# Half of the second batch's keys projected at the first batch's second norm, and the first attention begun with half of v

## The chip, the core and the metric

The kernel runs on one core of a Trainium2 chip. A core has five engines that work side by side, each through its own queue of instructions: TensorE (PE in the profile; its weight loads are PEld), VectorE (DVE), ScalarE (ACT), GpSimd (POOL) and SyncE (SP, which here only issues DMA transfers). They wait for one another by semaphores. The metric is the time of one execution on the device in microseconds (us). The kernel before took 3892.06 us in the median of three runs (3891.22 to 3893.94).

## What is computed

The input x has 8 batches of 1024 tokens (32 x 32) with 512 channels, in fp32. Two attention layers with a residual follow each other, each after a group norm over 32 groups of 16 channels and all tokens:

```python
# layer 0: 16 heads of 32 channels
qkv = _gn(x).reshape(B, N, C) @ w_qkv
attn = softmax((q * SCALE) @ k.T)           # per head, 1024 x 1024
x = x + (attn @ v) @ w_proj + b_proj
# layer 1: 4 heads of 128 channels, with relative positions
q, k, v = _gn(x) @ Wq * scale, _gn(x) @ Wk, _gn(x) @ Wv
attn = softmax(q @ k.T + rel_w + rel_h)     # the two terms come from q and pos_emb_w, pos_emb_h
x = x + (attn @ v) @ Wo
```

## The kernel before

**Products.** Every projection of a batch (512 x 512 weights times 512 channels x 1024 tokens) is done by a scheme with seven block products instead of eight (`seven`), twice per projection, for unit u = 0 and u = 1, each of which gives half of the output. So a projection is 14 products. One product is two chunks of 128 channels, each as four matmuls of 32 output columns side by side (`by_columns`, L312), for two halves where the output is in rows. The products of one unit come in the order `ORDER = [0, 5, 1, 4, 6, 2, 3]` and gather in three PSUM banks x, y and z; ACT copies two partial results into SBUF (p1, p7) and one out (c11), DVE does the adds a (L372), b (L380), c12 (L414) and c21 (L417), and POOL adds c22 (L421). The data side of the products are sums of quarters of x, made by `forms` (four DVE operations, L332 to L335): three of them lie in tiles of their own (`form1`, `form2`, `form4`, one buffer each), one in place. The weight side (differences of quarters of each weight matrix) is made once by `Matrix.add_up` (L146) and kept in DRAM; for the three matrices of the first batch's q, k and v it also stays in SBUF (`kept`).

**The stream of weights.** `Stream` follows a plan, a list of (matrix, rows or columns, unit). While a product of one unit runs, `ahead(i)` issues on SP the load of the same factor for the next unit, so weights are loaded seven products ahead (L194, L198).

**Attention 0** (`attention_0`) has 64 steps per batch: four groups of four heads, two halves of 512 queries, eight blocks j of 128 keys. `front` of a step does the scores of four heads into one PSUM tile ps, which has one buffer (L532), and ACT's exponential of it into e (L540, two buffers). `back` of the step before multiplies e with v into acc (L551) and adds e to the running sum es on DVE (L560 for the second block, L562 for the later ones). After the last block `finish` sums es over keys on PE (L572), and `normalise` turns it into reciprocals (L495 to L513) and multiplies q's place, where the output now lies, on POOL (L517).

**The order.** `side_by_side` runs attention 0 of batch b and, between its steps, draws the other work of the loop's turn b from a chain of generators in proportion to costs: a product counts 2, and a turn's `total` is spread over the 65 steps. In turn 0 this other work is `rest_of_first` (the second halves of q and k of batch 0), the loading and norm of batch 1 (`load`), and `before_0` of batch 1 (q, k, v: 42 products), with `other_sums`, the weight sums of five more matrices on POOL, put in after products 2, 9, 16, 23 and 30 of it. In turn 1 it is the output projection WP of batch 0 (`after_0`), its norm 1 (`norm_1`, with the scalings at L292), the projections of layer 1 (`second`), attention 1 (L647 to L670) and `before_0` of batch 2. Around the norm of turn 1 four entries of cost `ALONE = 4` are drawn with no product, and the first matmuls of `second` are kept in program order (`marked`). From turn 2 on, the norm lies between the products of WO of an older batch. What is drawn gives each instruction its rank; within an engine's queue an instruction can be put earlier when the ones ahead of it are not ready by the compiler's plan.

Before turn 0, `load_first` reads and norms batch 0, and `before_first` projects all of v and the first halves of q and k; only then the first attention begins.

**Room.** Large tiles (x, q, k, v, weight sums) share eight blocks of one pool (`BLOCKS = 8`).

Of the kernel before, what the change touches and what calls it, by code (L numbers as in the profile page):

```python
# [27 lines left out]
def quick_path(  # L28
# [138 lines left out]
    class Stream:  # L167
# [3 lines left out]
        def __init__(self, plan):  # L171
            self.plan = plan
            self.tiles = {}
            self.at = -1
            for i in ORDER:
                self.load(0, i)

        def load(self, n, i):
            if n >= len(self.plan):
                return  # L180
            m, rows, u = self.plan[n]
            if rows and u == 1:
                self.tiles[n, i] = self.tiles[n - 1, i]
                return
            got = []
            src = m.factor(i)
            if m.kept:
                got = [src[:, c, :] if rows else src[:, c, u * P : (u + 1) * P] for c in range(HC)]
                if i == ORDER[-1] and (u == 1 or rows):
                    m.kept = None  # L190
            elif rows:
                for c in range(HC):
                    t = mem.tile([P, HN], F32, tag="w", name=f"w_{m.name}_{n}_{i}_{c}", bufs=16)
                    nc.sync.dma_start(t, src[:, c, :])  # L194
                    got.append(t)
            else:
                t = mem.tile([P, HC, P], F32, tag="w", name=f"w_{m.name}_{n}_{i}", bufs=16)
                nc.sync.dma_start(t, src[:, :, u * P : (u + 1) * P])  # L198
                got = [t[:, c, :] for c in range(HC)]
            self.tiles[n, i] = got  # L200

        def unit(self, m, rows, u):
            self.at += 1
            assert self.plan[self.at] == (m, rows, u)

# [3 lines left out]

        def ahead(self, i):  # L210
            self.load(self.at + 1, i)

# [40 lines left out]

    def group_norm(st, xT, name, after=None):

# [35 lines left out]
        for cc in range(CC):  # L291
            nc.vector.tensor_scalar(  # L292
                xT[cc],
                xT[cc],
                mean[:, cc : cc + 1],
                rstd[:, cc : cc + 1],
                op0=ALU.subtract,
                op1=ALU.mult,
            )
            if cc % 2:  # L300
                yield 0


    in_place = [False]

    half_done = [None]

# [15 lines left out]

    def forms(x, name):


        a11, a12 = x[:, :HC, :NB], x[:, HC:, :NB]
        a21, a22 = x[:, :HC, NB:], x[:, HC:, NB:]
        s1, s2, s4 = [
            mem.tile([P, HC, NB], F32, tag=f"form{i}", name=f"f{i}_{name}", bufs=1) for i in (1, 2, 4)  # L330
        ]
        nc.vector.tensor_add(s1, a21, a22)  # L332
        nc.vector.tensor_sub(s2, s1, a11)
        nc.vector.tensor_sub(a21, a11, a21)
        nc.vector.tensor_sub(s4, a12, s2)  # L335
        return [a11, a12, s4, a22, s1, s2, a21]
# [4 lines left out]
    def seven(fs, u, rows, sink, name, hook=None):  # L341
# [4 lines left out]
        def product(out, i, start):  # L346
# [4 lines left out]
            else:  # L351
                for t in range(2):
                    for c in range(HC):
# [7 lines left out]
                        )  # L361
            stream.ahead(i)

# [7 lines left out]
        a = snapshot("es1", f"a_{name}")  # L371
        nc.vector.tensor_add(a, y, p1)  # L372
        sink.early(p1, a)
# [97 lines left out]

    def project_rows(fs, m, y, name, hook=None):

        for u in range(2):
            dst = [
# [42 lines left out]

    def attention_0(q, k, v, b):

        steps = [(m, h, j) for m in (0, 2, 1, 3) for h in range(NH) for j in range(NT)]
        state = {}
# [20 lines left out]
        def back(m, h, j, e):  # L543
            name = f"0_{b}_{m}_{h}_{j}"
            if j == 0:
                state["acc"] = psum.tile([P, NB], F32, tag="acc", name=f"acc_{name}", bufs=1)
                state["first"] = e
            acc = state["acc"]
            for r in range(HB):
# [4 lines left out]
                    e[:, r, :],  # L554
                    start=(j == 0),
                    stop=(j == NT - 1),
                )
            if j == 1:
                state["esum"] = mem.tile([P, HB, NB], F32, tag="es0", name=f"es_{name}", bufs=1)
                nc.vector.tensor_add(state["esum"], state["first"], e)  # L560
            elif j > 1:
                nc.vector.tensor_add(state["esum"], state["esum"], e)  # L562
            if j < NT - 1:
                return
# [193 lines left out]
    def before_first(st):  # L758

        fs = st["xn"]  # L760
        st["v"] = block("v0_0", [P, NT, C])
        yield from project_rows(fs, WV0, st["v"], "v0_0")
        st["q0"] = block("q0_0")
        st["q"] = chunks(st["q0"])
        st["k"] = chunks(block("k0_0"))
        yield from project_T(fs, WQ0, st["q"], "q0_0", (0,))
        yield from project_T(fs, WK0, st["k"], "k0_0", (0,))

    def rest_of_first(st):
# [4 lines left out]
    def before_0(b, st, hook=None):  # L774

        fs = st.pop("xn")
        st["q0"] = block(f"q0_{b}")
        st["q"] = chunks(st["q0"])
        yield from project_T(fs, WQ0, st["q"], f"q0_{b}")
        st["k"] = chunks(block(f"k0_{b}"))  # L780
        yield from project_T(fs, WK0, st["k"], f"k0_{b}")
        st["v"] = block(f"v0_{b}", [P, NT, C])
        yield from project_rows(fs, WV0, st["v"], f"v0_{b}", hook)

    def after_0(b, st, hook=None):

        fs = st.pop("ao0") if "ao0" in st else forms(st["q0"], f"ao0_{b}")
        x = st["x1"] = block(f"x1T_{b}")
# [9 lines left out]

    def norm_1(b, st, after=None):
        xT = chunks(st["x1"])  # L800
        st["kept"] = put_away(xT, f"1_{b}")
        yield from group_norm(st, xT, f"1_{b}", after)

# [57 lines left out]

    def side_by_side(first, rest, total):

        steps = CC * NH * NT + 1
        done = 0
        at = 0
        for _ in first:
# [25 lines left out]

    ALONE = 4

    WQ0, WK0, WV0 = [Matrix(w_qkv, i * C, f"qkv{i}") for i in range(3)]
    WP, WQ1, WK1 = Matrix(w_proj, 0, "p"), Matrix(Wq, 0, "q1"), Matrix(Wk, 0, "k1")
    WV1, WO = Matrix(Wv, 0, "v1"), Matrix(Wo, 0, "o")
    def units(m, rows=False):
        return [(m, rows, u) for u in range(2)]  # L900

    FIRST = units(WQ0) + units(WK0) + units(WV0, True)
    plan = units(WV0, True) + [(m, False, u) for u in range(2) for m in (WQ0, WK0)]
    for b in range(B + 1):
        if b >= 1:
            plan += units(WP)
        if b >= 2:
            plan += units(WO)
        if b >= 1:
            plan += units(WQ1) + units(WK1) + units(WV1, True)  # L910
        if b + 1 < B:
            plan += FIRST
    plan += units(WO)
# [22 lines left out]
    for b in range(B + 1):  # L936
# [11 lines left out]
        if last is not None:  # L948
            norm = norm_1(b - 1, last, (lambda: half_done[0]) if past is not None else None)
            rest.append(after_0(b - 1, last, forms_past if past is not None else None))  # L950
# [4 lines left out]
            else:  # L955
                rest.append(chain([ALONE], (cost + ALONE for cost in norm), marked()))
                total += 4 * ALONE
            rest.append(later(second, b - 1, last))
# [15 lines left out]
        if coming is not None:  # L974

            before = later(before_0, b + 1, coming, forms_0 if last is not None else None)
            rest.append(before if last is not None else woven(before, other_sums(), 2, 7))
            total += 3 * PRODUCT - (PRODUCT // 2 if last is not None else 0)
        if here is not None:
            side_by_side(attention_0(here["q"], here["k"], here["v"], b), chain(*rest), total)  # L980
# [495 lines left out]
```

## Time and profile before

| what | us |
|---|---|
| median of three runs | 3892.06 |
| span of the profiled execution | 3891.6 |
| PE busy / not busy in the span | 3809.4 / 82.2 |
| first matmul of the first projection | 25.66 |
| first scores of attention 0 of batch 0 | 79.08 |
| WP of batch 0 begins | 342.53 |
| layer 1's q of batch 0 begins | 420.20 |

In a line of the timeline the columns are start, duration, engine, line, operation, output and inputs, how often, and in brackets the idle time just before it and what ended it. In a line of a stretch they are its bounds, its length, and for each engine busy time and number of instructions, then the clock granted to TensorE (1.00 is full), the busy share of the DMA engines and GB/s. A line of waits has the total, the number and the longest.

### The profile page before, as it was taken

What the parts mean: (1) busy time and instruction counts of PE and PEld (TensorE: products, weight loads), DVE (VectorE), ACT (ScalarE), POOL (GpSimd) and SP (SyncE); (2) the same over time, 40 slices, a digit from 0 to 9 for tenths busy, and PEclk for the clock granted to TensorE, in tenths of its full rate; (3) what the DMA queues carried; (4) which work ended last, traced back from release to release, by engine and by line L of the source; (5) the groups of instructions that cost most, each with busy time, mean ns of one, the idle gap of its engine ahead of it and who ended that gap; (6) DMA issues with size and microseconds to landing.
All of it is one profiled execution on the core that took longest, in us unless ns stands there. A gap on an engine that the chain in (4) does not pass through costs nothing.

```text
span 3891.6 us, 79819 instructions
## 1 busy us (share of the span) xinstructions
PE 3809.4 (98%) x34478; PEld 1368.4 (35%) x34478; DVE 2515.8 (65%) x2905; ACT 1725.4 (44%) x1767; POOL 618.9 (16%) x400
## 2 busy tenths in 40 slices
PE   8999899999999999999999999999999999999998
PEld 3222244232442324432344323433234332334353
DVE  5767775577755867458674586646866568665544
ACT  2554553445435354344544445444453445553132
POOL 1341001121111210112110121111211112001101
PEclk9999999999999999999999999999999999999999
DMA  5231120133201422023220231202411033111401
GB/s 169 77 106 42 47 61 6 39 116 69 62 1 40 124 66 57 6 81 92 53 55 13 92 89 41 53 20 92 93 41 41 25 96 76 33 43 34 123 17 23
DMA packets 482984, 234.73 MB, mean 60 GB/s; under 512 B 269600, under 2 KB 461376, under 8 KB 481600
## 3 DMA queue, kind: packets, MB, share of 16 engines
q1 hardware_dynamic: 470992, 213.74, 20.4%
q0 software_dynamic: 2608, 13.70, 1.0%
q8 instruction: 274, 4.49, 0.5%
q10 hardware_dynamic: 9024, 2.10, 0.3%
q14 instruction: 86, 0.70, 0.1%
HBM read 170.72 MB, written 58.72 MB: 59 GB/s over the span
## 4 chain that ended last, share of the span: by engine, by line
PE 86%; DVE 7%; ACT 3%; issue 2%; POOL 1%; DMA 0%; SPq 0%; DVEq 0%; POOLq 0%; ACTq 0%
PE ps L532 12%; PE ps L647 11%; PE acc L659 11%; PE acc L551 10%; PE y_v L312 4%; PE y_k L312 4%; PE y_q L312 4%; PE ps L648 3%; PE x_v L312 3%; PE x_k L312 3%; PE x_q L312 3%; PE z_k L312 3%; PE z_v L312 3%; PE z_q L312 3%; ACT e L540 2%; DVE es L562 2%
## 5 line engine op out<-in xcount | busy, mean ns | idle before, releaser
L540 ACT ACTIVATE e<-ps 128x2048 f32<-128x2048 f32 x512 | 961.7, 1878 | 838.1 <-PE ps L532 624.0
L562 DVE TENSOR_TENSOR es<-es,e 128x2048 f32<-128x2048 f32 x384 | 892.1, 2323 | 422.7 <-ACT e L540 420.1
L532 PE MATMUL ps<-q,k 32*64 32x512 f32 x8192 | 577.1, 615 | 27.4 <-ACT e L540 27.4
L650 ACT ACTIVATE e<-ps 128x512 f32<-128x512 f32 x512 | 306.0, 598 | 572.2 <-PE ps L648 538.9
L551 PE MATMUL acc<-e,v 128*32 128x512 f32 x4096 | 547.3, 606 | 0.0
L647 PE MATMUL ps<-q,k 128*128 128x512 f32 x1024 | 525.0, 594 | 0.3 <-DVE posT L633 0.3
L659 PE MATMUL acc<-e,v 128*128 128x512 f32 x1024 | 521.9, 592 | 0.0
L517 POOL TENSOR_TENSOR q<-q,su 128x512 f32<-128x512 f32 x128 | 213.3, 1666 | 1596.1 <-DVE su L513 1551.3
L670 DVE TENSOR_TENSOR es<-es,e 128x512 f32<-128x512 f32 x384 | 290.7, 757 | 251.0 <-ACT e L650 248.9
L648 PE MATMUL ps<-posT,sel 128*128 128x512 f32 x512 | 406.7, 794 | 0.0
L647 PEld LDWEIGHTS ps<-q,k 128*128 128x128 f32 x1024 | 192.5, 190 | 251.2 <-issue 244.8
L532 PEld LDWEIGHTS ps<-q,k 32*64 32x64 f32 x8192 | 120.3, 130 | 422.7 <-issue 220.5
L659 PEld LDWEIGHTS acc<-e,v 128*128 128x128 f32 x1024 | 193.1, 189 | 146.8 <-issue 105.2
L551 PEld LDWEIGHTS acc<-e,v 128*32 128x32 f32 x4096 | 81.5, 108 | 413.2 <-issue 366.2
L560 DVE TENSOR_TENSOR es<-e,e 128x2048 f32<-128x2048 f32 x64 | 174.3, 2723 | 38.4 <-ACT e L540 38.4
L497 DVE STREAM_TRANSPOSE tu<-su 128x512 f32<-128x512 f32 x128 | 90.6, 708 | 128.8 <-ACT su L495 128.7
L495 ACT COPY su<-sums 128x512 f32<-128x512 f32 x128 | 75.1, 586 | 150.7 <-PE sums L572 78.0
L648 PEld LDWEIGHTS ps<-posT,sel 128*128 128x128 f32 x512 | 97.3, 190 | 122.5 <-issue 122.5
L633 DVE TENSOR_TENSOR posT<-pp,posT 32x512 fp32r<-32x512 f32 x128 | 112.0, 875 | 32.1 <-ACT posT L628 30.8
L668 DVE TENSOR_TENSOR es<-e,e 128x512 f32<-128x512 f32 x64 | 44.2, 690 | 134.8 <-ACT e L650 134.8
L421 POOL TENSOR_TENSOR k<-b_k,p_k 128x512 f32<-128x512 f32 x32 | 51.1, 1598 | 482.0 <-ACT p_k L386 480.0
L628 ACT CAST posT<-pp 32x512 fp32r<-32x512 f32 x128 | 106.0, 828 | 45.9 <-PE pp L615 44.8
(195 smaller groups left out, 4457.4 us busy)
## 6 DMA issues: line engine op xcount, KB each, us to landing
w_qkv<-ws_qkv SPq DMA_DIRECT2D x168, 128.0 KB, 2.5
d<-x0T SPq DMA_DIRECT2D x32, 512.0 KB, 3.5
x1T<-d SPq DMA_DIRECT2D x32, 512.0 KB, 5.2
d<-x1T SPq DMA_DIRECT2D x32, 512.0 KB, 3.6
x2T<-d SPq DMA_DIRECT2D x32, 512.0 KB, 6.1
w_qkv<-in_L_conv_w_qkv SPq DMA_DIRECT2D x126, 128.0 KB, 2.2
out<-ot SPq DMA_DIRECT2D x240, 64.0 KB, 2.0
xs<-in_x SPq DMA_DIRECT2D x224, 64.0 KB, 2.6
```

The lines of the kernel that those rows point to most:

```text
L312: ins = nc.tensor.matmul(out[columns, :], weights[:, columns], moving, start=start, stop=stop, skip_group_check=open_sum,)
L517: nc.gpsimd.tensor_tensor(dst, dst, su, op=ALU.mult)
L532: nc.tensor.matmul(ps[some, r, :], k[m][rows, j * P + 64 * i : j * P + 64 * i + 64], q[m][rows, h * NB : (h + 1) * NB], start=True, stop=True,
L540: nc.scalar.activation(e, ps, AF.Exp, scale=D0 ** -0.5)
L551: nc.tensor.matmul(acc[r * D0 : (r + 1) * D0, :], v[:, j, c0 : c0 + D0], e[:, r, :], start=(j == 0), stop=(j == NT - 1),)
L560: nc.vector.tensor_add(state["esum"], state["first"], e)
L562: nc.vector.tensor_add(state["esum"], state["esum"], e)
L647: nc.tensor.matmul(ps, k[h][:, keys], q[:, h, queries], start=True, stop=False)
L648: nc.tensor.matmul(ps, sel_flat[:, keys], posT[:, h, queries], start=False, stop=True)
L650: nc.scalar.activation(e, ps, AF.Exp, scale=1.0 / math.sqrt(D1))
L659: nc.tensor.matmul(acc, v[:, j, h * D1 : (h + 1) * D1], e, start=(j == 0), stop=(j == NT - 1),)
L670: nc.vector.tensor_add(state["esum"], state["esum"], e)
```

## The change

The plan of the stream now lists for every unit which factors it loads, and `ahead()` loads the next one of a flat list of all uses. The second half of v of batch 0 is no longer projected ahead of the first attention but between its first four steps, two products per step; in these four steps nothing else is drawn (`alone`), and all of batch 0 takes the key blocks in the order 0, 1, 4, 5, 2, 3, 6, 7. `before_0` of batch 1 leaves out the second half of k; this is projected in turn 1 after WP, with the norm of batch 0 woven between its products in place of the `ALONE` entries, and the norm's four scalings are queued on DVE behind the last add a (`begun`). Since x of batch 1 is still in use then, the forms of batch 0's attention output get a block in place of the form tiles.

```diff
         def load(self, n, i):
-            if n >= len(self.plan):
-                return
-            m, rows, u = self.plan[n]
-            if rows and u == 1:
+            m, rows, u, some = self.plan[n]
+            if rows and u == 1 and not m.kept:
                 self.tiles[n, i] = self.tiles[n - 1, i]
                 return
...
-        def ahead(self, i):
-            self.load(self.at + 1, i)
+        def ahead(self):
+            use = next(self.uses, None)
+            if use is not None:
+                self.load(*use)
...
-            nc.vector.tensor_scalar(
-                xT[cc],
-                xT[cc],
-                mean[:, cc : cc + 1],
-                rstd[:, cc : cc + 1],
-                op0=ALU.subtract,
-                op1=ALU.mult,
-            )
+            with tc.issue_after(behind().ins) if behind is not None else nullcontext():
+                nc.vector.tensor_scalar(
+                    xT[cc],
+                    xT[cc],
+                    mean[:, cc : cc + 1],
+                    rstd[:, cc : cc + 1],
+                    op0=ALU.subtract,
+                    op1=ALU.mult,
+                )
...
-    def forms(x, name):
+    def forms(x, name, room=None):
...
+        if room is not None:
+            s1, s2, s4 = [room[:, i, :].rearrange("p (c n) -> p c n", n=NB) for i in range(3)]
...
-        nc.vector.tensor_add(a, y, p1)
+        begun[0] = nc.vector.tensor_add(a, y, p1)
...
-        yield from project_rows(fs, WV0, st["v"], "v0_0")
+        yield from project_rows(fs, WV0, st["v"], "v0_0", units=(0,))
...
+    def attention_first(st):
+
+        values = project_rows(st["xn"], WV0, st["v"], "v0_0", units=(1,))
+        steps = attention_0(st["q"], st["k"], st["v"], 0, [0, 1, 4, 5, 2, 3, 6, 7])
+        for at, cost in enumerate(steps):
+            if at < NT // 2:
+                for _ in range(2):
+                    next(values, None)
+            yield cost
...
-        yield from project_T(fs, WK0, st["k"], f"k0_{b}")
+
+        yield from project_T(fs, WK0, st["k"], f"k0_{b}", (0,) if b == 1 else (0, 1))
...
+    def other_keys(b, st):
+        yield from project_T(st["xn"], WK0, st["k"], f"k0_{b}", (1,))
...
-        fs = st.pop("ao0") if "ao0" in st else forms(st["q0"], f"ao0_{b}")
+        fs = st.pop("ao0") if "ao0" in st else forms(st["q0"], f"ao0_{b}", block(f"forms_{b}"))
...
-    def side_by_side(first, rest, total):
-
-        steps = CC * NH * NT + 1
+    def side_by_side(first, rest, total, alone=0):
+
+
+        steps = CC * NH * NT + 1 - alone
         done = 0
-        at = 0
+        at = -alone
...
-    ALONE = 4
...
-            norm = norm_1(b - 1, last, (lambda: half_done[0]) if past is not None else None)
+            if past is not None:
+                norm = norm_1(b - 1, last, after=lambda: half_done[0])
+            else:
+                norm = norm_1(b - 1, last, behind=lambda: begun[0])
...
-                rest.append(chain([ALONE], (cost + ALONE for cost in norm), marked()))
-                total += 4 * ALONE
+                rest.append(chain(woven(other_keys(b, here), norm, 0, 1), marked()))
+                total += PRODUCT // 2
...
-            total += 3 * PRODUCT - (PRODUCT // 2 if last is not None else 0)
-        if here is not None:
+            total += 3 * PRODUCT - PRODUCT // 2
+        if b == 0:
+            side_by_side(attention_first(here), chain(*rest), total, NT // 2)
+        elif here is not None:
             side_by_side(attention_0(here["q"], here["k"], here["v"], b), chain(*rest), total)
```

## The prediction

> **What bounds the kernel now.** I read the page's engine table first, then the waits of the TensorE, then the start in stretches, and at last the order of instructions around the longest wait.
>
> ```profile
> PE 3809.4 (98%) x34478; PEld 1368.4 (35%) x34478; DVE 2515.8 (65%) x2905; ACT 1725.4 (44%) x1767; POOL 618.9 (16%) x400
> ```
> TensorE (PE) is busy for all but 82 us of a span of 3891.6. The diff neither adds nor removes a matmul, so it can only win or lose idle time and time at a low clock. Everything it moves lies ahead of 425 us. The waits of PE from 79 to 345 us (attention 0 of batch 0), then from 390 to 421 (norm 1 of batch 0):
>
> ```profile
> PE ps L532 <- ACT e L540: 8.8, 10, 2.2
> PE y_k L312 <- DVE b_k L380: 2.3, 1, 2.3
> PE y_q L312 <- DVE a_q L372: 2.1, 1, 2.1
> ...
> PE ps L532 <- ACT e L540: 12.0, 6, 7.6
> ```
> The columns are total us, times, longest. Stretches (length, busy time of PE, PEld, DVE, ACT, POOL, clock, DMA) of the projections ahead of the first attention, of the norm, of what follows it, and of the like norm one batch later:
>
> ```profile
> 55.10:79.15 24.05, 24.05 (x234) 7.66 (x226) 9.30 (x15) 3.52 (x6) 2.56 (x2) 1.00 0.19 30
> ...
> 390.00:420.00 30.00, 18.02 (x184) 3.38 (x180) 26.96 (x33) 12.36 (x8) 2.43 (x3) 0.83 0.17 62
> 420.00:450.00 30.00, 30.00 (x312) 7.57 (x308) 17.67 (x17) 16.04 (x13) 2.56 (x2) 1.00 0.14 40
> ...
> 838.00:895.00 57.00, 54.30 (x572) 13.68 (x568) 52.29 (x62) 25.46 (x20) 18.45 (x11) 1.00 0.39 93
> ```
> PE loses 12.0 us in the norm of batch 0, nothing before the attention and nothing after. Why, in order of time:
>
> ```profile
> 396.71 1.04 POOL L289 TENSOR_TENSOR rstd<-var,neg_half 128x4 f32<-128x4 f32 x1 [1.26 <-DVE var L285]
> 397.79 2.26 DVE L292 TENSOR_SCALAR x1T<-x1T,back,rstd 128x1024 f32<-128x1024 f32 x3 [1.16 <-POOL rstd L289]
> 399.96 2.29 DVE L560 TENSOR_TENSOR es<-e,e 128x2048 f32<-128x2048 f32 x1
> 402.35 1.88 ACT L540 ACTIVATE e<-ps 128x2048 f32<-128x2048 f32 x1 [7.82 <-DVE es L560]
> 404.27 2.01 PE L532 MATMUL ps<-q,k 32*64 32x512 f32 x16 [7.58 <-ACT e L540]
> ...
> 411.97 1.12 PE L532 MATMUL ps<-q,k 32*64 32x512 f32 x16 [1.06 <-ACT e L540]
> ```
> The sum es stands behind the norm's small operations, the wait for POOL and three scalings; e has two buffers, so ACT waits for es and PE for ACT. Two more steps at 1.04 us show the plain price of a step with no projection in it: ps and acc take 1.04 + 1.00, but the next ps must wait for the exponential of 1.88.
>
> [...] after 7.58 us idle ps takes 2.01 instead of 1.11, and PE's clock is 0.50 from 403 to 409 us; waits of 1.06 do no harm. [...] es was ready at 394.53, when its e ended, and began at 399.96.
>
> **Part 1, v.** One product of the Strassen-like seven is 1.72 us of PE (16 matmuls of 512 columns, or 32 of 256). The second half of v is seven products, 42.84 to 54.9: 12.05 us. They leave the path ahead of the attention, where PE had no gap, and go two per step into its first four steps. There a step is 2.04 + 3.44 = 5.5 us against some 2.4 on ACT (1.88 and three copies of 0.59 in 3.5 steps) and 3.1 on DVE (2.29 and four adds of 0.69), so PE does not wait; it pays these 12.05 there. Net 0: only a move. No DMA moves with it: these weights lie in SBUF. The new order of blocks (0, 1, 4, 5, then 2, 3, 6, 7) first needs the second half at step 4; it is done at step 3.
>
> **Part 2, half of k.** Seven products (12.05 us) leave attention 0 of batch 0. Filler there falls from 56 products over 65 steps to 49 over the 61 left after the first four. In the order of PE's instructions the 42 products of q and k fill steps 0 to 41, one each, and the 14 of v the next 22.4 at 20 of 32 matmuls each: 64.4 of 65. Now 35 + 22.4 = 57.4 of 61: three more steps empty, at 1.05 each, +3.2 us. Bounds: 0, if the order spreads the filler thinner (a step with 20 matmuls of v is 3.33 us and still covers the 3.15 of ps, exponential and waits), and 6, if the sums at the borders of a head make each such step worse (1.1 to 1.7 in v's part now). I take 3.2. The loads of these weights, seven of 128 KB on SP, move with them, still seven uses ahead, some 12 us against 2.5 to land.
>
> **Part 3, the norm.** From the end of WP (390.46) to x_q (420.20) PE now does 7 steps and one set of sums. Lost there: 11.98 idle (30.00 - 18.02) and, at half clock, 0.9 in ps at 404.27, 0.9 in the acc behind it (1.94 against 1.06) and 0.4 in the next ps: 14.2 us. The padding of four times 4 units goes and k's seven products take its place, so that 12.05 us of work lie in these gaps. The four scalings are held behind k's first DVE add, a_k, so es, ready earlier, can pass them. What remains: DVE had 26.96 of 30 busy; with one step less (-2.29) and k's four adds (4 x 0.69) it has 27.4 against PE's 0.87 + 6 x 2.04 + 12.05 = 25.2. The surplus is the last two forms operations (2 x 1.22), which only WQ1's later products need. One batch on, with 14 products of WO in the norm, PE lost 57.00 - 54.30 = 2.7: 1.3 for ps behind the scalings, 1.4 for y_wo waiting for a_wo. The second cannot come here if a_k goes ahead of the scalings. I take 1.3; bounds 0 and 4 (2.7 and half a step).
>
> The held scalings have es and k's adds queued behind them on DVE, and behind es ACT's next exponential; that is the 1.3.
>
> **Part 4, room.** The forms of batch 0's attention output now go to a block of their own, since x of batch 1 and its form tiles stay alive until k is done. The same four DVE operations: 0. Of eight blocks, seven are held near the end (x0T, v, q, k, and q, k, v of batch 1); prep_o and x1T share the eighth as before (x1T loaded at 278.7, just after prep_o was stored), and forms can have k's block, free from the last ps on, 4 us before they begin at 345.62. Cost 0, at worst 2. The stream of weights is rewritten, but stays seven uses ahead: 0. Later batches: 0.
>
> **Sum.** -12.05 (ahead) + 12.05 (first steps) - 12.05 + 3.2 (rest of the attention) + 12.05 - 14.2 + 1.3 (norm) = -9.7 us. On the span of 3891.6 this gives 3881.9; the three runs have the median 3892.06, 0.46 above the span, so 3882.4.
>
> **Rivals.** *More is won.* Three hiccups in 79 to 220 us cost 2.2, 2.1 and 2.3 idle and twice 1.7 at half clock, 10.0 in all. The first is es behind batch 1's own scalings at 101.6, which could fall into the 5.5 us steps; the others follow 22 us of POOL additions for the weight sums. If two go: 3882.4 - 6 = 3876. Against it: all three causes remain in the program, only shifted.
>
> *Most is eaten.* DVE, at 27.4 of 25.2, is the bound in the norm: es falls behind scalings and adds again and half the loss stays, 7 instead of 1.3: 3888. For it speaks DVE's 52.29 of 57 in the like norm; against it that PE still ran 54.30 there.
>
> *Slower.* POOL adds up five weight matrices in attention 0; p and q came as a pair, 153.7 to 176.3, 22.6 us without a gap. before_0 is now 35 products, not 42, so the last sum, prep_o, is put at step 59 instead of 51, and prep_v at 50. If the pair v and o starts just ahead of the last normalising product on POOL (L517 at 344.32), the forms and WP wait up to 22.6: 3882.4 + 22.6 = 3905. It decides from 17.5 us of delay on, that is, if it starts within some five steps of the end. Against it: prep_o's additions began at step 44, seven ahead of its place, and ended 70 us before that L517.
>
> **Chances.** Forecast 0.52, more won 0.17, eaten 0.17, slower 0.14. About 0.2% (7.8 us, so 3884.3 and 3899.8) is what a measurement of this kernel tells from no change. The forecast's own range, 3878 to 3887, has 0.06 above that line: faster 0.46 + 0.17 = 0.63, same 0.06 + 0.17 = 0.23, slower 0.14. The range: from all three hiccups gone (9.7 + 10 is 3872.4) to the eaten case with 3 us more, 3873 to 3891.
>
> **What would show it.** Right: the first ps near 67 us instead of 79.08; ps intervals near 5.5 in the first four steps; no wait above 2 us and no half clock in the norm, k's products between sums and x_q; three steps with waits near 1.05 at the end of the attention. Wrong: a wait of y_wp above 3.5, prep_o's additions beside the last L517, or es behind the scalings with ACT waiting over 3 us.

## The result and the profile after

The changed kernel took **3876.89 us** in the median of four runs (3874.85 to 3877.31); the kernel before took 3891.64 beside it (3886.99 to 3893.94). The ratio is 0.9963, with a 95% interval from 0.9945 to 0.998: faster by 14.75 us, where 9.7 were forecast. Two more sets of runs gave ratios of 0.9963 [0.9949, 0.9977] and 0.9964 [0.9952, 0.9976]. The profiled execution has a span of 3875.2 us against 3891.6.

The engine table of the kernel after, which answers to the first line shown of before:

```profile
PE 3803.0 (98%) x34478; PEld 1375.0 (35%) x34478; DVE 2516.4 (65%) x2905; ACT 1723.9 (44%) x1767; POOL 625.1 (16%) x400
```

The matmuls are the same 34478. Idle time of PE fell from 82.2 to 72.2 us, and busy time by 6.4, with a granted clock of 0.95, 1.00 and 0.96 in the three stretches below where it was 0.92, 0.98 and 0.89. Where, is read from stretches cut at the same events in both kernels: first product of the projections, first ps, first y_wp of WP, x_q of layer 1. First the kernel before, then the kernel after (bounds, length, busy time of PE, PEld, DVE, ACT, POOL, clock, DMA share, GB/s):

```profile
25.66:79.08 53.42, 52.72 (x673) 23.66 (x673) 23.16 (x33) 7.04 (x12) 5.70 (x5) 0.92 0.41 107
79.08:349.20 270.12, 253.30 (x2760) 68.21 (x2757) 197.56 (x162) 144.83 (x106) 84.79 (x49) 0.98 0.26 82
349.20:420.20 71.00, 59.02 (x572) 13.42 (x576) 57.54 (x61) 29.83 (x20) 8.82 (x8) 0.89 0.16 55
```

```profile
27.28:67.32 40.04, 39.02 (x448) 20.40 (x448) 20.30 (x29) 5.27 (x9) 4.43 (x4) 0.95 0.50 130
67.32:333.51 266.19, 251.54 (x2885) 71.65 (x2883) 196.10 (x162) 143.77 (x106) 81.35 (x48) 1.00 0.24 76
333.51:400.81 67.30, 65.45 (x647) 16.15 (x650) 55.52 (x61) 29.70 (x22) 16.14 (x10) 0.96 0.26 87
```

| stretch | before | after | difference | forecast |
|---|---|---|---|---|
| start, to the first product | 25.66 | 27.28 | +1.6 | 0 |
| projections ahead of attention 0 | 53.42 | 40.04 | -13.4 | -12.05 |
| attention 0 of batch 0 | 270.12 | 266.19 | -3.9 | +3.2 |
| WP and norm, to x_q | 71.00 | 67.30 | -3.7 | -0.85 with the next row |
| all that follows | 3471.40 | 3474.39 | +3.0 | |
| sum | 3891.6 | 3875.2 | -16.4 | -9.7 |

The last two rows belong together: PE does 14 attention steps ahead of x_q now and did 15 before, so a step of some 3 us passed into the rest; -0.7 in all. A product of WP has changed sides as well: before, 16 matmuls of x_wp lie ahead of the first y_wp, after, 32. So the rows of the attention and of the norm are safest read as one sum with the last: -4.6, where +2.35 was forecast. The start is not touched by the diff and lies between 25.7 and 27.4 in all the profiles of this case. What is off is mainly the attention: 7.1 us better than forecast in its row.

The waits of PE in the kernel after, first in attention 0, then in WP and the norm (total, times, longest):

```profile
PE ps L539 <- ACT e L547: 10.3, 8, 2.9
PE sums L579 <- DVE es L569: 1.8, 1, 1.8
...
PE y_wp L315 <- DVE forms L340: 2.5, 1, 2.5
PE ps L539 <- ACT e L547: 1.8, 1, 1.8
```

In the norm the waits of 12.0 us (longest 7.6) have become one of 1.8. The timeline of the kernel after shows why:

```profile
379.87 2.28 DVE L567 TENSOR_TENSOR es<-e,e 128x2048 f32<-128x2048 f32 x1
380.03 3.03 POOL L290 TENSOR_TENSOR rstd<-var,neg_half 128x4 f32<-128x4 f32 x1 [1.26 <-DVE var L286]
382.25 1.88 ACT L547 ACTIVATE e<-ps 128x2048 f32<-128x2048 f32 x1 [3.02 <-DVE es L567]
384.17 1.12 PE L539 MATMUL ps<-q,k 32*64 32x512 f32 x16 [1.85 <-ACT e L547]
...
386.36 0.68 DVE L379 TENSOR_TENSOR a_k<-y_k,p_k 128x512 f32<-128x512 f32 x1
386.96 2.98 DVE L294 TENSOR_SCALAR x1T<-x1T,back,rstd 128x1024 f32<-128x1024 f32 x4
```

The sum es goes first, the four scalings wait behind a_k, and ps takes 1.12 us where it took 2.01; the granted clock from 384 to 386 us is 1.00, where it was 0.50 from 403 to 409 us before. What is left of the wait has another source: the exponential that es needs ended at 377.84, and es still stood behind the small operations of the norm until 379.87.

### The profile page after: what moved, and what is told of

It is laid out like the page before. It is cut to its first block, busy times and chain, and to the rows that moved or that the text cites. A ratio compares the mean times of both kernels' runs of the same rounds, so it can differ in the third digit from the quotient of the medians.

```text
span 3875.2 us, 79813 instructions
## 1 busy us (share of the span) xinstructions
PE 3803.0 (98%) x34478; PEld 1375.0 (35%) x34478; DVE 2516.4 (65%) x2905; ACT 1723.9 (44%) x1767; POOL 625.1 (16%) x400
## 4 chain that ended last, share of the span: by engine, by line
PE 87%; DVE 8%; ACT 2%; issue 2%; DMA 0%; SPq 0%; POOL 0%; DVEq 0%; ACTq 0%; POOLq 0%
PE ps L539 12%; PE ps L654 11%; PE acc L666 11%; PE acc L558 11%; PE y_q L315 4%; PE y_v L315 4%; PE y_k L315 4%; PE ps L655 3%; PE x_q L315 3%; PE z_k L315 3%; PE x_v L315 3%; PE x_k L315 3%; PE z_q L315 3%; PE z_v L315 3%; DVE es L569 2%; ACT e L547 2%
```

## The experiments

Each of the single-part kernels is shown as its edit against the changed kernel; "..." stands for lines left out. The kernel before ran beside them in each of the three sets: its medians were 3891.31 in the first (the whole change again and the single parts), 3888.8 in the second (the hold left out, the hold in all batches, WP in its place) and 3891.03 in the third (the rest). The whole change was in the first and the third.

### The same kernel twice more

> The changed kernel once more, beside the others, on their chip. All theories: 14 to 16 us below the kernel before (the forecast said 9.7, the first runs 14.75).

> The whole change again, for the comparison on one chip: 3875 to 3877.5 us, ratio to the kernel before 0.996.

Measured: 3876.67 us (3875.15 to 3878.0) against 3891.31, and 3876.9 (3871.31 to 3878.2) against 3891.03. The attention took 266.18 and 266.22 us, PE's two longest waits in it were 2.91 and 1.82 at the same steps, WP and norm took 67.04 and 67.19: the account above is not that of one odd execution.

### The shift of v alone

```diff
...
-        yield from project_T(fs, WK0, st["k"], f"k0_{b}", (0,) if b == 1 else (0, 1))
+        yield from project_T(fs, WK0, st["k"], f"k0_{b}")
...
-        fs = st.pop("ao0") if "ao0" in st else forms(st["q0"], f"ao0_{b}", block(f"forms_{b}"))
+        fs = st.pop("ao0") if "ao0" in st else forms(st["q0"], f"ao0_{b}")
...
-                norm = norm_1(b - 1, last, behind=lambda: begun[0])
+                norm = norm_1(b - 1, last)
...
-                rest.append(chain(woven(other_keys(b, here), norm, 0, 1), marked()))
-                total += PRODUCT // 2
+                rest.append(chain([4], (cost + 4 for cost in norm), marked()))
+                total += 16
...
```

> Only part 1: the second half of v between the first four steps; all of batch 1's k is projected in attention 0 of batch 0 as before, and the norm has its four entries of padding again. Theory 1 (the gain is PE work put into the gap of the norm; v's move is a move of 12.05 us): the norm still loses some 14, the first attention has 3 more steps' worth of work than steps, which runs over its end into the wait for the forms (3.5 idle and about 2.8 at half clock now): 2 to 6 us below before. Theory 2 (the gain is the earlier start of the attention): 12 to 15 below before. Theory 3 (the gain beyond the forecast is a matter of which short waits in the first attention happen to remain): about 5 below before, with the norm unchanged.

Measured: 3881.02 us (3879.61 to 3884.16), ratio 0.9974 [0.9963, 0.9984], -10.3. Attention 0 and the norm in the stretches of this kernel:

```profile
68.11:339.94 271.83, 256.20 (x2981) 72.70 (x2979) 202.19 (x166) 145.95 (x109) 85.72 (x50) 1.00 0.26 82
339.94:411.02 71.08, 59.09 (x574) 13.43 (x578) 57.56 (x61) 29.83 (x20) 8.84 (x8) 0.89 0.16 55
```

The norm is that of before (71.08 against 71.00). The attention took in 12.05 us of products and grew by 1.7. "Net 0: only a move" does not hold: moving v won some 10 us by itself, which lies between what the theories said (2 to 6, about 5, 12 to 15).

### Half of k alone

```diff
-        yield from project_rows(fs, WV0, st["v"], "v0_0", units=(0,))
+        yield from project_rows(fs, WV0, st["v"], "v0_0")
...
-        if b == 0:
-            side_by_side(attention_first(here), chain(*rest), total, NT // 2)
-        elif here is not None:
+        if here is not None:
```

> Only parts 2 and 3: all of v ahead of the attention as before, half of batch 1's k in the norm. Theory 1: the norm wins some 12, but attention 0 of batch 0 has 49 products for 65 steps, of which 57.4 are filled; 7 empty steps at 1.05, less one or two that WP's first product can fill: 5 to 8 lost; 4 to 8 us below before. Theory 2: no gain, 0 to 2. Theory 3: 12 to 14 below before, with the empty steps costing nothing.

Measured: 3883.71 us (3881.33 to 3886.16), ratio 0.9982 [0.9974, 0.999], -7.6. Its attention 0 and norm:

```profile
79.21:341.77 262.56, 243.02 (x2664) 65.19 (x2661) 192.41 (x158) 142.78 (x103) 83.31 (x47) 0.99 0.26 81
341.77:407.90 66.13, 64.27 (x644) 16.00 (x648) 56.70 (x61) 29.71 (x22) 14.11 (x10) 0.98 0.22 70
```

The norm gains as in the whole change. The attention, freed of 12.05 us, shrank by only 7.6. The gains of the two parts, 10.3 and 7.6, come to 17.9, where the whole change gained 14.6 in the same set of runs.

### Half of k computed in both places

Only half of k is moved, v is not, and that half of k is also still computed in attention 0: seven products done twice, 12.05 us of PE more than before.

```diff
-        yield from project_rows(fs, WV0, st["v"], "v0_0", units=(0,))
+        yield from project_rows(fs, WV0, st["v"], "v0_0")
...
-        yield from project_T(fs, WK0, st["k"], f"k0_{b}", (0,) if b == 1 else (0, 1))
+        yield from project_T(fs, WK0, st["k"], f"k0_{b}")
...
-            plan += FIRST if b else units(WQ0) + units(WK0)[:1] + units(WV0, True)
+            plan += FIRST
...
```

> The price of k's seven products at their new place alone: the kernel before, with the second half of batch 1's k projected in attention 0 of batch 0 as before and then once more, into the same place, in the norm of batch 0 (12.05 us of PE work added and nothing taken away; forms in their own block, scalings held). Theory 1: the gap pays for it: within 3 us of before. Rival (the gap closes by itself or VectorE is the bound there, so that the products cost what they take): 8 to 12 us above before.

Measured: 3889.59 us (3882.72 to 3894.64), ratio 0.9996 [0.9988, 1.0004]. Its norm, with the seven products in it:

```profile
348.81:417.27 68.46, 66.60 (x660) 16.42 (x664) 55.44 (x61) 29.71 (x22) 14.09 (x10) 0.96 0.22 70
```

Twelve microseconds of matmuls were put into the norm at no measured cost; PE is busy 66.60 us there instead of 59.02. The stretch is 2.5 us shorter, with one attention step of some 3 us less in it, so the products cost it about half a microsecond. So the norm of before held that much room, and the forecast's term of 14.2 us lost was of the right size.

### What the parts have in common: the hiccups

The parts did not add up by their work: v put in 12.05 and cost 1.7, k took out 12.05 and gave 7.6. I therefore went through attention 0 step by step, from one ps to the next. In the part with products of q and k a regular step takes 3.76 us, with the sums of a head 4.62; both are the same in all kernels. What a step takes above that, where one of the long waits lies in it or matmuls at a lower clock follow (before, at 108.63, acc takes 1.70 us instead of 1.06; the mean clock from 107 to 111 us is 0.74), I call a hiccup. Short waits in this part, up to 0.75 us each and 2.2 to 3.2 us in all, stand in every one of these kernels and are left out, and so are the borders of heads among the products of v.

| kernel | hiccups, us above a regular step | their sum | attention 0 | without them |
|---|---|---|---|---|
| before | 2.22 + 1.70; 3.17; 4.66 + 0.33 + 0.37 | 12.45 | 270.12 | 257.7 |
| half of k twice | 2.22 + 1.64; 3.17 + 1.63; 3.38 | 12.04 | 269.32 | 257.3 |
| after | 2.99; 2.01 | 5.00 | 266.19 | 261.2 |
| half of k alone | 2.21 + 1.70; 3.17 | 7.08 | 262.56 | 255.5 |
| v alone | 1.84; 1.87; 2.01; 2.02 | 7.74 | 271.83 | 264.1 |

Before lost 12.45 us this way, after loses 5.00: 7.45 less. Without them the attention grew from 257.7 to 261.2, by 3.5, where 3.2 were forecast. So in these profiles the miss of the attention, 7.1 us, is about that of the hiccups.

That the two numbers meet so closely hides two smaller terms. The stretch "after" has a product of WP more in it, and the wait of the first y_wp at its end fell from 3.50 to 2.50 us. With WP kept in its place (a run below), the attention without its hiccups (5.02) took 260.5, 2.8 more than before, so its filler, the products between the steps, added 3.8 and the shorter wait took 1.0 off.

The timeline of the kernel before shows the three of them, and at last the wait for the forms:

```profile
101.59 1.77 DVE L292 TENSOR_SCALAR x0T<-x0T,back,rstd 128x1024 f32<-128x1024 f32 x1 [1.22 <-POOL rstd L289]
103.28 2.28 DVE L562 TENSOR_TENSOR es<-es,e 128x2048 f32<-128x2048 f32 x1
107.58 1.12 PE L532 MATMUL ps<-q,k 32*64 32x512 f32 x16 [2.16 <-ACT e L540]
108.63 1.70 PE L551 MATMUL acc<-e,v 128*32 128x512 f32 x8
...
178.16 0.69 DVE L372 TENSOR_TENSOR a_q<-y_q,p_q 128x512 f32<-128x512 f32 x1 [3.34 <-POOL q L421]
178.91 1.04 PE L312 MATMUL y_q<-f_xn,w_qkv 128*32 128x512 f32 x2 [2.13 <-DVE a_q L372]
...
210.91 6.12 DVE L562 TENSOR_TENSOR es<-es,e 128x2048 f32<-128x2048 f32 x1 [1.47 <-ACT e L540]
211.13 3.75 POOL L146 TENSOR_TENSOR prep_v<-prep_v 128x512 f32<-128x512 f32 x3
216.96 0.68 DVE L380 TENSOR_TENSOR b_k<-y_k,p_k 128x512 f32<-128x512 f32 x1
217.69 0.64 PE L312 MATMUL y_k<-f_xn,w_qkv 128*32 128x512 f32 x1 [2.33 <-DVE b_k L380]
...
345.54 1.26 POOL L431 TENSOR_TENSOR x1T<-x1T,p_wp 128x512 f32<-128x512 f32 x1
345.62 2.27 DVE L332 TENSOR_TENSOR f_ao<-q 128x1024 f32<-128x1024 f32 x1 [1.45 <-POOL q L517]
```

First: es behind batch 1's own scaling, which waits for POOL; then ps waits, and acc takes 1.70 instead of 1.06. Second: a_q waits 3.34 us for an addition of POOL, which came behind the last additions of the weight sums p and q there (they ended at 176.0 us). Third: es takes 6.12 us instead of 2.28, because three additions of POOL (3.75 us) run in it; 3.75 + 2.28 is 6.03, so the lengths are those of two engines that do this work one after the other. Then b_k is late and PE waits. Last: the first form of batch 0's output takes 2.27 us beside an addition of POOL. In the kernel after, POOL has no addition there, the form takes 1.23, and y_wp waits 1.0 us less. In the profile es begins 0.22 us ahead of the additions and ends 2.15 us after the last of them; why these took their turn inside it was not shown.

The same places and the two remaining hiccups in the kernel after:

```profile
87.33 2.28 DVE L569 TENSOR_TENSOR es<-es,e 128x2048 f32<-128x2048 f32 x1
90.55 2.98 DVE L294 TENSOR_SCALAR x0T<-x0T,back,rstd 128x1024 f32<-128x1024 f32 x4 [0.33 <-POOL rstd L290]
...
142.24 2.00 DVE L342 TENSOR_TENSOR f_xn<-x0T,f_xn 128x1024 f32<-128x1024 f32 x1
144.17 2.28 DVE L567 TENSOR_TENSOR es<-e,e 128x2048 f32<-128x2048 f32 x1
148.47 1.12 PE L539 MATMUL ps<-q,k 32*64 32x512 f32 x16 [2.92 <-ACT e L547]
...
163.38 9.38 DVE L569 TENSOR_TENSOR es<-es,e 128x2048 f32<-128x2048 f32 x2
163.55 3.75 POOL L146 TENSOR_TENSOR prep_q<-prep_q 128x512 f32<-128x512 f32 x3
172.90 1.06 PE L579 MATMUL sums<-es,ones 128*32 128x512 f32 x8 [1.82 <-DVE es L569]
```

With v's products in the first steps, batch 1's norm falls right behind the long steps; there an es stands ahead of the scalings while POOL makes rstd, and no step is late. POOL's additions still hit es (9.38 us for two, which are 4.56 at 2.28 each), but at the end of a head, where only the sums wait. The 2.99 is new: es behind batch 1's forms.

### Is it the order that costs? Batch 1's scalings held, with half of k alone

```diff
...
-                nc.vector.tensor_add(state["esum"], state["esum"], e)
+                last_es[m, h, j] = nc.vector.tensor_add(state["esum"], state["esum"], e)
...
+        held = iter((4, 5, 6, 7))
...
-        yield from group_norm(st, xT, f"0_{b}")
+        yield from group_norm(st, xT, f"0_{b}", behind=(lambda: last_es[0, 0, next(held)]) if b == 1 else None)
...
```

> Only half of k is moved, as in the run with k alone, but batch 1's own four norm scalings now stand singly behind the fifth to eighth sum es of the first head, where they stood in front of the fifth and sixth. Theory (the sum behind these scalings cost the run with k alone a wait of 2.15 us at 107.7 us and half clock of some 1.7 after it, and the shift of v in the whole change is what removed that): attention 0, 262.6 us there, gets 3 to 4 us shorter, 258.6 to 259.6, and there is no ps wait above 1.2 us and no ps of 2 us between 100 and 116 us. Rival (the stretch is limited by the whole of VectorE's or PE's work there and the wait only comes back later, or the half clock is the chip's own choice): attention 0 stays within 1 us of 262.6.

Measured: attention 0 took 260.47 us, 2.1 shorter, not 3 to 4. At the place of the first hiccup the timeline now reads:

```profile
108.91 1.12 PE L540 MATMUL ps<-q,k 32*64 32x512 f32 x16 [0.33 <-ACT e L548]
109.96 1.06 PE L559 MATMUL acc<-e,v 128*32 128x512 f32 x8
...
114.08 1.07 PE L580 MATMUL sums<-es,ones 128*32 128x512 f32 x8 [1.33 <-DVE es L570]
```

The wait of 2.15 fell to 0.33, and acc took 1.06 us instead of 1.78: the order made the first hiccup. But half came back one step on: the scalings now stand between the last sums es, and the head's sums wait 1.33 us. The hiccups add up to 0.39 + 1.54 + 3.19 = 5.12, and the attention without them is 255.4, as without the hold (255.5). Over the whole kernel it cannot be told apart: 3883.26 us (3880.71 to 3886.7) against 3883.71, as WP and norm took 67.97 instead of 66.13: after the same wait of ps there, 1.85 us here and 1.86 there, matmuls ran slower behind it in this profile alone (acc 1.89 us and x_k 2.84 here, 1.07 and 1.90 there; clock of the stretch 0.95 and 0.98).

### The norm without the hold

The whole change, but the four scalings of batch 0's norm 1 are not held behind a_k.

```diff
-                norm = norm_1(b - 1, last, behind=lambda: begun[0])
+                norm = norm_1(b - 1, last)
```

> The changed kernel without the hold of the four scalings behind k's add a. VectorE's order then has three scalings ahead of the first sum es again, as before the change; everything else stays. Theory 1 (the hold lets es pass, so that ACT's next exponential isn't late): ACT waits for es some 5 us again, PE has k's products for part of it: 2 to 6 us above the changed kernel. Rival (k's products fill the gap whatever VectorE's order is): within 1 us of it.

Measured: 3881.21 us (3879.13 to 3884.35), ratio 0.998 [0.9973, 0.9987]. That is 4.5 above the run with the hold in all batches, told next, which took 3876.75 beside it. Against the kernel before it gains 7.6, the whole change gained 14.1 and 14.6 in its own sets; so the hold is worth 4.5 to 7.0. The timeline of its norm, and the stretch of WP and norm:

```profile
378.99 2.26 DVE L294 TENSOR_SCALAR x1T<-x1T,back,rstd 128x1024 f32<-128x1024 f32 x3 [1.16 <-POOL rstd L290]
381.16 2.28 DVE L567 TENSOR_TENSOR es<-e,e 128x2048 f32<-128x2048 f32 x1
...
385.47 2.01 PE L539 MATMUL ps<-q,k 32*64 32x512 f32 x16 [5.27 <-ACT e L547]
```

```profile
332.41:404.26 71.85, 66.58 (x646) 16.25 (x650) 58.97 (x64) 29.71 (x22) 13.17 (x10) 0.93 0.24 81
```

Three scalings pass ahead of es again, ps waits 5.27 instead of 1.85 and takes 2.01 instead of 1.12; the stretch is 4.6 us longer. The products of k alone would not have been enough; the order of DVE is worth some 4.5 of the norm's gain.

### The hold in the later batches too

```diff
-                norm = norm_1(b - 1, last, after=lambda: half_done[0])
+                norm = norm_1(b - 1, last, after=lambda: half_done[0], behind=lambda: begun[0])
```

> The changed kernel with the same hold in the later turns too: there two of the four scalings of the norm go behind WO's second add a, TensorE's order is the same. If the waits of those turns (1.3 for ps, 1.4 for y_wo, six times) come from es and a_wo standing behind the scalings: 1 to 2.5 us less in each, 5 to 12 us below the changed kernel. Rival (VectorE's total, 52 of 57 us, is what binds there): within 2 us of it.

Measured: 3876.75 us (3875.89 to 3877.85), ratio 0.9969 [0.9958, 0.998], no gain over the whole change. In the norm of the next batch the waits of PE are

```profile
PE ps L539 <- ACT e L547: 1.3, 1, 1.3
PE y_wo L315 <- DVE a_wo L379: 1.0, 1, 1.0
PE y_wo L315 <- DVE b_wo L387: 0.3, 1, 0.3
```

against 1.0 for ps and 1.4 for y_wo without it. With 14 products of WO in the norm only 2.4 to 2.6 us were lost there, and the order only shares them out anew.

### WP's first product kept in its place

The three steps forecast as empty did not show: in the kernel after, x_wp, the first two products of WP in the order of PE, fills the last steps of the attention in pieces. Here they are kept in the written order.

```diff
+            if past is None:
+                rest.append(marked())
             rest.append(after_0(b - 1, last, forms_past if past is not None else None))
```

> The changed kernel with WP's first product kept behind everything ahead of it in program order, so that it can't fill the last steps of the first attention. The forecast's three empty steps should then show: three waits of ps near 1.05 at the end of the attention; the product then lies in the wait for the forms, which gets shorter by up to its 1.72. Theory 1: 0.5 to 3 us above the changed kernel. Rival (the empty steps cost nothing since the exponential is hidden otherwise): no such waits, within 0.5.

Measured: 3873.45 us (3872.36 to 3877.38), ratio 0.9962 [0.9948, 0.9975]: not slower, where 0.5 to 3 us more were expected, and not told apart from the whole change (3876.67 in its own set) or from the run with the hold in all batches. The empty steps are there in its timeline:

```profile
317.03 1.12 PE L539 MATMUL ps<-q,k 32*64 32x512 f32 x16 [0.18 <-ACT e L547]
320.18 1.12 PE L539 MATMUL ps<-q,k 32*64 32x512 f32 x16 [1.04 <-ACT e L547]
...
327.78 1.92 PE L315 MATMUL x_wp<-q,w_p 128*32 128x512 f32 x16
```

Steps of 3.15 us with waits of 0.18 and 1.04, and one more of 1.04 for acc. They cost next to nothing, because the first x_wp then lies ahead of the last ps, where PE waits 2.02 us in the kernel with half of k alone, whose x_wp went into earlier steps; y_wp waits 2.50 in all three. The attention took 265.54 us against 266.19, with a product of WP less in it, and the stretch behind it 68.35 against 67.30: together 333.89 against 333.49.

### The last form put later, and with it WP in its place

Two of the four form operations of batch 1's x are issued later, and the last one is queued behind the first sum es of the third head.

```diff
...
-        nc.vector.tensor_sub(a21, a11, a21)
-        nc.vector.tensor_sub(s4, a12, s2)
+        if late is None:
+            nc.vector.tensor_sub(a21, a11, a21)
+            nc.vector.tensor_sub(s4, a12, s2)
+        else:
+            late += [(a21, a11, a21), (s4, a12, s2)]
...
-        yield from project_T(fs, WQ0, st["q"], f"q0_{b}")
+        def late():
+            for at, operands in enumerate(st.pop("late") or []):
+                with tc.issue_after(last_es[2, 0, 1].ins) if at else nullcontext():
+                    nc.vector.tensor_sub(*operands)
+                yield 0
+
+        yield from woven(project_T(fs, WQ0, st["q"], f"q0_{b}"), late(), 1, 2)
```

> The whole change, and the last form of batch 1's x is queued on VectorE behind the first sum es of the third head, which stood behind it and began at 144.17 us. Theory (the wait of ps of 2.92 us at 148.47 is this order and nothing else): es begins 2 us earlier, the wait falls to 0.9 to 1.1, attention 0 takes 264.2 us or a little less where the whole change took 266.2, and the time is 2 us below the whole change. Rival (another wait takes its place, such as the form's product waiting for the form): within 0.5 us of the whole change.

> The run with the last form put later and, with it, the first product of WP kept in its place in the written order instead of among the last steps of attention 0. Theory (the two edits touch different places and add up; the second alone gave 3873.45 beside 3876.75 of the whole change in one set of runs, but that lay within their spread): 2 to 5 us below the whole change, about 3872. Rival (the second edit is worth nothing and its 3 us were spread): 2 us below the whole change, as with the form alone.

The 3876.75 that the second of these texts gives to the whole change was that of the run with the hold in all batches.

Measured with the form alone: 3874.47 us (3874.2 to 3876.0), ratio 0.996 [0.9947, 0.9974], 2.4 below the whole change in the same set; attention 0 took 265.00. The timeline of it:

```profile
141.70 1.28 POOL L528 TENSOR_TENSOR q<-q,su 128x512 f32<-128x512 f32 x1 [2.98 <-DVE su L524]
142.05 3.07 DVE L571 TENSOR_TENSOR es<-e,e 128x2048 f32<-128x2048 f32 x1
147.15 1.12 PE L543 MATMUL ps<-q,k 32*64 32x512 f32 x16 [1.78 <-ACT e L551]
```

The wait fell from 2.92 to 1.78, not to 1: es now runs beside a multiplication on POOL and takes 3.07 instead of 2.28. The attention gained 1.2 of the 2 us expected. With both edits the time was 3873.34 us (3870.63 to 3875.22), ratio 0.9958 [0.9944, 0.9971], the lowest of all, 3.6 below the whole change on the same chip; the intervals overlap, so that it beats the whole change is likely but not shown. In its profile the wait of y_wp, 2.51 us, was followed by a y_wp of 1.93 us, that of 2.50 in the whole change by one of 3.64 (clock 0.50 from 333 to 338 us), so not all of the 3.6 need be the work of the edits.

## Why the prediction was right in its sign and short in its size

**Ahead of the attention: right.** -12.05 forecast, -13.4 measured in this profile. The stretch itself varies: 52.1 to 53.4 us in the four profiles with v as before, 40.0 to 41.9 in the nine with half of it. Of the first four steps only two came to 5.49 as forecast; the first has no acc yet (4.64), and seven products leave one for the fourth (3.77).

**Part 3, the norm: right in its mechanism, 1.3 us too good in its size.** -0.85 was forecast and -0.7 measured together with what follows, but this has a product of WP less in it. The two kernels with WP in its place have 68.46 and 68.35 us in this stretch, 2.5 to 2.65 below before, and with the step of 3 us counted that is +0.4 to +0.5. 1.3 was taken for what remains; ps waits 1.85. The reason given for it, es and the adds behind the held scalings, is not what the trace shows: es stands ahead of the scalings and behind the norm's small operations, 2.0 us late. That k's products are free there and that the order on DVE matters are both shown, by the half of k computed twice and by the run without the hold. The rival "most is eaten", with 7 us remaining, is out.

**Part 1, v: the step that failed.** It said "Net 0: only a move", and the rival that more is won was set aside with "all three causes remain in the program, only shifted". The causes did remain, but what a hiccup costs depends on where it meets the steps: 12.45 us before, 5.00 after. So the rival "more is won", given 0.17, is what came, and not the forecast: the first and the third hiccup are gone, the weight sums that made the second cost 2.01 at another place, and a new one of 2.99 came. The first, 3.92 us, went because of v's move: it is gone with v alone and with the whole change, it stays with half of k alone, and putting es ahead of the scalings by hand removes that wait too. The second, 3.17, keeps the same company: it stays in the three kernels with v as before and half of k moved, while with v alone and in the whole change the same sums of p and q meet es at the end of a head and cost 2.01. The third goes with half of k, not with v: before, the weight sums of k and v come as a pair, loaded at 191.8 and 192.6 us, and cost 5.36, 3.38 in the kernel with half of k twice and 2.02 in that with v alone. Where those seven products have left the attention, the load of the second sum comes some 30 us after the first (191.9 and 220.3 with half of k alone, 209.6 and 242.0 in the kernel after), and this hiccup is missing. For the second and the third these are readings of five kernels side by side; no run moved POOL's additions alone. The remaining ones, of batch 1's forms, were tried once, by the last form put later. Which hiccups a shift of the program brings up was not forecast from the profile before.

I had also sized the hiccups too small: 10.0 where a step-by-step reading of the same trace gives 12.45. The second was counted at its wait alone, 2.1, and costs 3.17 from ps to ps; the third at 2.3 and 1.7, and costs 5.36.

**Part 2, the attention's filler: right as a sum by luck, wrong by parts.** +12.05 - 12.05 + 3.2 was forecast, +3.5 measured without hiccups (+3.8 with WP in its place and the wait of y_wp apart). But neither part alone moved what I booked for it: without hiccups v alone added 6.4 (264.1 - 257.7), not 12.05, and half of k alone took away 2.2 (257.7 - 255.5), not 8.85. The reason lies in the steps: an empty one takes 3.15 us, one with 20 matmuls of v, 1.08 us of work, 3.33, one with a product of 1.72 takes 3.76. ps must wait for the exponential of 1.88 us, so the first 1.1 us of work in a step is almost free: 0.18 us here. Seven products of k fewer make seven steps of 3.76 into 3.15, a gain of 4.3 by this count (7 x 0.61) rather than 12. Even this is more than the 2.2 measured; x_wp, which fills four of these steps there, takes a part of it back, and the rest was not traced. The two errors cancelled since filler left and came in the same attention. The empty steps cost less than said, and by another way: x_wp filled them, and where it does not, x_wp takes a wait at the end of the attention.

**Part 4, room: no cost, as said, and 1.0 us won.** y_wp waits 2.50 for the forms, 3.50 before, since the first form no longer runs beside an addition of POOL (1.23 us instead of 2.27). The kernel with v alone, with the forms' room as before, keeps the wait (3.49) and the addition. The slower rival, weight sums on POOL in front of the last normalising product, did not come: the additions of prep_o ended at 276.5 us, the last normalising product began at 329.7.

The measured 3876.89 lies inside the range of 3873 to 3891 and next to the 3876 of the rival "more is won"; that the two agree to 1 us is partly chance, since -1.0 at the wait of y_wp and +1.3 in the norm, which the rival has not, offset each other.

## What to carry to other kernels

A move of work by "net 0" has a second effect: it shifts every stall of the stretch against the steps it falls on (12.45 us of hiccups became 5.00 here), and those are to be priced one by one, from the start of one step to the start of the next, with what follows them. Where a step has a floor (here 3.15 us, scores and exponential), price filler by the length of the step with and without it, not by its own work. A sum that frees a buffer should stand ahead of a norm's scalings in the queue that both share: this order alone was worth 4.5 us or more here. It is no rule, though: in the later norms it gave nothing, and for batch 1's scalings 2.1 us in the attention and nothing in the whole.

## What the runs showed of the hardware that I had not expected

**After the same wait the clock fell in some profiles and not in others.** Six profiles of kernels that are alike up to that place have the same wait of 2.9 us, which ends at 148 to 149 us. Over the 6 us from 147 us the mean clock was 1.00 in four of them and 0.72 in two (without the hold, and with it in all batches), which took them about 1.7 us by an estimate (0.28 x 6). In the kernel after, ps then took 1.12 us, as shown above; without the hold it took 2.02:

```profile
147.78 2.02 PE L539 MATMUL ps<-q,k 32*64 32x512 f32 x16 [2.92 <-ACT e L547]
```

So the length of the wait alone did not decide it. Slow matmuls followed waits of 7.58 us (before: ps 2.01, at 404.27) and 5.27 (without the hold: ps 2.01), but also of 2.50 (y_wp 3.64 in the kernel after, 1.93 after 2.51 with both edits), 2.16 (before, at 107.58: acc 1.70) and 1.85 (batch 1's scalings held, at 388.59: acc 1.89; in the kernel after, at 384.17, 1.07). The prediction's own rival counted half clock after waits of 2.2 and 2.3. What did decide it was not shown. And the lower clock was not all loss: in the two profiles with it the later wait of the sums (1.82 us) is missing, so that their hiccups add up to 4.53 and 4.68 against 5.00.

**A sum es on DVE and POOL's operations beside it took longer, either way round.** Where es passes ahead of the norm's scalings in the kernel after, POOL's tiny rstd, 1.04 us before and without the hold, takes 3.03: it starts 0.16 us after es and ends 0.9 after it. In the kernel before, an es with three of POOL's additions beside it takes 6.12 instead of 2.28, and one at 207.12 takes 2.33, while the addition that began 0.13 us after it takes 3.34; three additions of prep_qkv at 12.92, beside DVE's statistics of the norm, took 3.71 together.
